# Beginning the second pair's value loads three places sooner in a macaron block with local attention

## The chip, the cores and the metric

The kernel runs on one core of a Trainium2 chip. The metric is the device time of one execution in microseconds (us), lower is better. A measured time is the median of several executions; beside it stands one execution that the hardware profiler recorded, from which every duration below comes.

A core has five engines with a queue of instructions each: PE (TensorE, matrix products; its weight loads are listed as PEld), DVE (VectorE), ACT (ScalarE), POOL (GpSimd) and SP (SyncE, which in this kernel only issues DMA transfers). Each works through its own queue in order, and waits where an instruction needs what another has not finished. Sixteen DMA engines carry out the transfers.

## The reference

The input is four sequences of 4096 rows of 512 numbers in float32. Each goes through three residual stages, with a layer norm ahead of each:

```python
x = x + 0.5 * ffn(layernorm(x))          # rows and weights rounded to a 6-bit grid per 32 numbers
x = x + attention(layernorm(x))
x = x + 0.5 * ffn(layernorm(x))
```

The attention has 16 heads of 32 numbers. Each row attends to the 13 rows around it only (at the ends of a sequence, to the 13 nearest the end), with a bias that depends on the relative position:

```python
attn = einsum('bhld,bhlkd->bhlk', q, k[nbr]) + rpb[:, bidx]
out = einsum('bhlk,bhlkd->bhld', softmax(attn), v[nbr])   # then out @ proj_w.T + proj_b
```

## The kernel before

**Tiles, groups, steps.** The rows are 128 tiles of 128. Four tiles make a group, so there are 32 groups, eight to a sequence. A float32 factor of a product is kept as two float16 parts, high and low, and a product is three sweeps of four matmuls of 128x512 (`product`, line 151): 12 matmuls. One step of the steady part does one tile of each stage, for different tiles: the first half-step `ffn` and the second (PSUM tiles `pmf`), the values (`pmv`), a quarter of a group's queries and keys (`pmqk`, two products), the scores (`ps`, line 433), the weighted sums (`pv`, line 503) and the output projection (`pmo`).

**Slots.** The order of the work is written out by hand. `begin(slot, stage, rank)` puts a stage in a slot; `run_slot` runs the stages of a slot by rank and moves each to its next slot, as its `yield slots, rank` says. A step is `STEP = 7` slots. What a stage emits in a slot goes to the end of the engines' queues, so slots and ranks alone set the order in every queue, SP's included.

**Scores and values.** The queries of a group are cut in blocks of 30; a block sees 42 keys. A block's probabilities, with high and low parts side by side, are transposed by a DMA (`pT<-p`, line 485) and multiplied with stacked values: 42 rows of v high, again v high, and v low, one over the other, for each block. [...] v goes through DRAM: `values` (line 299) computes a tile of v, ACT and DVE split it into `vt` (lines 310 and 311), and SP writes it out (`vd<-vt`, line 312). Once a group's rows are in DRAM, `load_stack` (line 394) reads them back, block by block (`vs<-vd`, line 409). It is called twice for a group: a pair is the 256 columns of eight heads, so pair 0 and pair 1 together are a group's 512 columns. A call issues three DMAs (high, high, low), or six in the first and last group of a sequence, where a block at the end breaks the even spacing. The pool `vsp` has two buffers; pair 1 of a group takes the one of pair 1 of the group before, so its loads wait until PE has read that.

**What else SP issues in a step.** Three transposes, one after another: `pT<-p`, `xT<-hlq` (line 205; the quantised rows for an `ffn` product, both halves together) and `x<-hln` (line 205; the normed rows for queries, keys and values). Then the write of v, the output of a finished tile (`out_dram<-x`, line 555) and the load of a new input tile (line 176). Each DMA of SP counts on one of eight semaphores in turn, so it also waits for the DMA eight places ahead of it to have landed.

**Where the two calls of `load_stack` stand.** Pair 0 is begun in slot 6*7+4 after the group's start, rank 9: behind the transposes of that step. Pair 1 is begun in slot 8*7, rank 9: the slot in which the next step's `values` stage issues its write of v, with rank 7.

Below, a group's four steps are counted from the first score matmul of each: pair 0's loads are issued near the end of the first step, pair 1's at the change from the second step to the third.

Of the kernel before, what the change touches and what calls it, by code (L numbers as in the profile page):

```python
# [64 lines left out]
def macaron_kernel(  # L65
# [96 lines left out]
    def begin(slot, stage, rank=5):  # L162
        slots.setdefault(slot, []).append((rank, stage))
# [395 lines left out]
    STEP = 7  # L559
# [6 lines left out]
    def one(f, *args):  # L566
        f(*args)
        return
        yield
# [22 lines left out]
    for t in range(NT):  # L592
        k = t * STEP
# [16 lines left out]
    for m in range(n_items):  # L610
        k = m * STEP
# [3 lines left out]
    for n in range(n_batch * NG):  # L615
        k = n * GROUP * STEP
        b, g = divmod(n, NG)
        begin(k + 6 * STEP + 4, one(load_stack, b, g, 0), 9)
        begin(k + 8 * STEP, one(load_stack, b, g, 1), 9)


    with tc.tile_pool(name="setup", bufs=1) as sp, tc.tile_pool(name="scratch", bufs=2) as scr:
# [289 lines left out]
```

## Time and profile before

| | |
|---|---|
| time before, median of 3 runs | 2408.76 us (2407.12 to 2414.85) |
| the profiled execution's own time | 2401.24 us |
| its span in the profile | 2399.4 us |
| granted TensorE clock, mean | 0.993 |
| busy: PE, DVE, POOL, ACT | 95%, 84%, 83%, 55% |
| DMA traffic | 360.58 MB, 150 GB/s in the mean |
| loads of stacked values (`vs<-vd`) | 144 of 357.0 KB, 24 of 378.0 KB, 24 of 315.0 KB, 48 of 21.0 KB |

The span is the profiler's stretch from the first to the last instruction. An entry such as "pmf<-wt,xT" names the tile written and those read. A wait is put down to what ended it; "issue" means that the profile shows nothing that the engine waited for. The chain of waits follows the work that ended last back to its beginning. In a timeline of SP, the length is the time that SP took to issue the DMA, not the transfer. The trace also holds each DMA packet and each increment of a DMA's semaphore, from which a landing time is read.

### The profile page before, as it was taken

The page shows a single profiled execution, that of the slowest core. Times are in us where ns is not written, and L with a number is a line of the kernel's source. Part 1 is how long each engine was busy: PE and PEld are TensorE (multiplying, and loading weights), DVE is VectorE, ACT ScalarE, POOL GpSimd, SP SyncE. Part 2 cuts the span into 40 slices and gives each one's busy share as a digit, 9 for nine tenths or more (in the row PEclk, how much of TensorE's full clock was granted, in tenths as well). Part 3 has the DMA queues.
Part 4 walks back from the last instruction along what each step waited for, and adds up shares of the span by engine and source line. Part 5 has one row for each costly group of instructions (what it writes and reads, how often), then busy time and mean ns, then how long its engine had stood idle before and what let it go on. Part 6 is the DMA issues. An engine that isn't in the chain of part 4 may idle for free.

```text
span 2399.4 us, 82333 instructions
## 1 busy us (share of the span) xinstructions
PE 2278.8 (95%) x35539; PEld 1114.0 (46%) x35539; DVE 2015.3 (84%) x3588; ACT 1327.1 (55%) x2080; POOL 1989.0 (83%) x2012
## 2 busy tenths in 40 slices
PE   0799999999999999999999999999999999999987
PEld 0244444444444444444444444444444444444442
DVE  8789888888888888888888888888888888888775
ACT  4455555555555556555555555555555555555442
POOL 5578888888888888888888888888888888888677
PEclk9899999999999999999999999999999999999998
DMA  5788888787787877778867778777778887777753
GB/s 153 145 150 153 158 164 158 148 157 151 145 161 156 152 150 159 146 153 162 161 145 156 150 146 167 153 154 147 159 139 156 158 158 146 162 148 143 137 115 90
DMA packets 925700, 360.58 MB, mean 150 GB/s; under 512 B 718876, under 2 KB 889752, under 8 KB 925336
## 3 DMA queue, kind: packets, MB, share of 16 engines
q1 hardware_dynamic: 924992, 354.79, 75.6%
q8 instruction: 278, 4.55, 0.8%
q10 hardware_dynamic: 344, 0.53, 0.1%
q14 instruction: 86, 0.70, 0.1%
HBM read 110.15 MB, written 67.29 MB: 74 GB/s over the span
## 4 chain that ended last, share of the span: by engine, by line
PE 89%; DVE 4%; DMA 3%; issue 1%; POOL 1%; ACT 1%; SPq 0%; DVEq 0%; ACTq 0%; POOLq 0%
PE pmqk L151 27%; PE pmf L151 26%; PE pmo L151 14%; PE pmv L151 13%; PE ps L433 6%; PE pv L503 3%; DMA xT<-hlq 2%; DVE hlq L204 0%; DVE fw L749 0%; DMA x<-hln 0%; DVE qk L373 0%; DVE stn L180 0%; POOL x L564 0%; ACT ring L530 0%; DVE whl L779 0%
## 5 line engine op out<-in xcount | busy, mean ns | idle before, releaser
L151 PE MATMUL pmf<-wt,xT 128*128 128x512 f16 x3048 | 703.1, 381 | 17.8 <-DMA xT<-hlq 17.7
L151 PE MATMUL pmqk<-x,wt 128*128 128x512 f16 x3072 | 707.7, 380 | 6.2 <-DMA x<-hln 5.4
L151 PEld LDWEIGHTS <-xT 128*128 128x128 f16 x3048 | 297.0, 98 | 386.1 <-DMA xT<-hlq 29.3
L151 PEld LDWEIGHTS <-wt 128*128 128x128 f16 x3072 | 290.0, 98 | 343.1 <-issue 9.7
L151 PE MATMUL pmv<-wt,x 128*128 128x512 f16 x1536 | 353.8, 380 | 5.1 <-DMA x<-hln 5.1
L151 PE MATMUL pmo<-wt,ring 128*128 128x512 f16 x1536 | 355.3, 381 | 2.6 <-issue 2.6
L246 POOL TENSOR_TENSOR yq<-yq,r 128x1024 f32<-128x1024 f32 (+1 forms) x141 | 246.2, 1746 | 130.8 <-DVE r L244 130.8
L564 POOL TENSOR_TENSOR x<-x,half_ffn_b 128x512 f32<-128x512 f32 x256 | 327.4, 1279 | 0.1
L275 DVE SCALAR_TENSOR_TENSOR x<-pmf,coef,x 128x512 f32<-128x512 f32 x256 | 179.5, 701 | 165.2 <-PE pmf L151 164.7
L530 ACT ACTIVATE ring<-pv 128x510 f16<-128x510 f32 (+8 forms) x224 | 82.3, 414 | 400.5 <-PE pv L503 400.5
L310 ACT CAST vt<-pmv 128x512 f16<-128x512 f32 x128 | 74.9, 585 | 389.3 <-PE pmv L151 389.3
L180 DVE BATCH_NORM_STATS2 stn<-x 128x6 f32<-128x512 f32 x384 | 265.3, 691 | 8.9 <-DMA x<-in_L_attn_x_dram 0.2
L251 POOL TENSOR_TENSOR yq<-q,sc 128x1024 f32<-128x1024 fp8e4 (+1 forms) x141 | 246.7, 1749 | 0.4 <-ACT q L249 0.4
L151 PEld LDWEIGHTS <-x 128*128 128x128 f16 x1536 | 150.5, 98 | 187.6 <-DMA x<-hln 5.6
L373 DVE SCALAR_TENSOR_TENSOR qk<-pmqk,qk_b,qk 128x512 f16<-128x512 f32 x256 | 190.6, 744 | 53.8 <-ACT qk L369 53.0
L476 POOL TENSOR_TENSOR sf<-sf,total 128x714 f32<-128x714 f32 (+2 forms) x128 | 178.6, 1395 | 44.2 <-DVE total L474 25.0
L151 PEld LDWEIGHTS <-ring 128*128 128x128 f16 x1536 | 140.2, 98 | 161.5 <-issue 4.2
L186 POOL TENSOR_SCALAR rsq<-mv 128x2 f32<-128x2 f32 (+1 forms) x141 | 131.3, 931 | 96.0 <-DVE mv L181 93.8
L249 ACT ACTIVATE q<-yq,nudge 128x1024 fp8e4<-128x1024 f32 (+1 forms) x141 | 149.9, 1063 | 108.0 <-POOL yq L246 99.8
L369 ACT ACTIVATE qk<-pmqk,qk_b 128x512 f16<-128x512 f32 x256 | 176.1, 688 | 53.2 <-PE pmqk L151 52.1
L233 ACT ACTIVATE yq<-x,nbq,rsq 128x512 f32<-128x512 f32 x254 | 193.0, 804 | 20.8 <-POOL nbq L192 20.2
L467 POOL TENSOR_TENSOR sf<-sf,top 128x714 f32<-128x714 f32 (+2 forms) x128 | 180.4, 1409 | 20.0 <-DVE top L465 19.8
(145 smaller groups left out, 3466.9 us busy)
## 6 DMA issues: line engine op xcount, KB each, us to landing
vs<-vd SPq DMA_DIRECT2D x144, 357.0 KB
x<-in_L_attn_x_dram SPq DMA_DIRECT2D x128, 256.0 KB
vd<-vt SPq DMA_DIRECT2D x128, 256.0 KB
out_dram<-x SPq DMA_DIRECT2D x128, 256.0 KB
vs<-vd SPq DMA_DIRECT2D x24, 378.0 KB
vs<-vd SPq DMA_DIRECT2D x24, 315.0 KB
rows<-in_L_attn_qkv_w_dram SPq DMA_DIRECT2D x12, 256.0 KB
xT<-hlq SPq DMA_TRANSPOSE x141
```

The source lines that it names most:

```text
L151: nc.tensor.matmul(pm, lhs(a, c), rhs(b, c), start=(n == 0), stop=(n == 3 * KC - 1))
L180: nc.vector.bn_stats(st, xs[t])
L233: nc.scalar.activation(y[:, u], xs[t], AF.Identity, bias=nb[:, u : u + 1], scale=rs[:, u : u + 1])
L246: nc.gpsimd.tensor_tensor(yb, yb, bc(r, QB), ALU.mult)
L249: nc.scalar.activation(q8, y, AF.Identity, bias=nudge, saturate=False)
L251: nc.gpsimd.tensor_tensor(yb, q8.rearrange("p u (n q) -> p (u n) q", q=QB), bc(sc, QB), ALU.mult)
L275: nc.vector.scalar_tensor_tensor(xs[t], pm, cf, xs[t], ALU.mult, ALU.add)
L369: nc.scalar.activation(t[:, s, 0, KN:], pms[s], AF.Identity, bias=bias)
L373: nc.vector.scalar_tensor_tensor(t[:, s, 1, KN:], pms[s], bias, t[:, s, 0, KN:], ALU.add, ALU.subtract)
L467: nc.gpsimd.tensor_tensor(s, s, bc(top[:, :n], KN), ALU.subtract)
L476: nc.gpsimd.tensor_tensor(s, s, bc(total[:, :n], KN), ALU.mult)
L564: nc.gpsimd.tensor_tensor(xs[t], xs[t], b, ALU.add)
```

## The change

The call of `load_stack` for pair 1 is begun in slot 7*7+4 after the group's start instead of slot 8*7. Rank, loads, buffers and all other stages are as they were.

```diff
         k = n * GROUP * STEP
         b, g = divmod(n, NG)
         begin(k + 6 * STEP + 4, one(load_stack, b, g, 0), 9)
-        begin(k + 8 * STEP, one(load_stack, b, g, 1), 9)
+        begin(k + 7 * STEP + 4, one(load_stack, b, g, 1), 9)
```

In SP's queue the order of a group's third step's beginning changes from `pT, xT, hln, vd, vs vs vs, out, x` to `pT, xT, hln, vs vs vs, vd, out, x`, with these names for the transposes of probabilities, quantised rows and normed rows, the write of v, the three loads, the output and the input load.

## The prediction

> **What bounds the kernel now.** The page first: its span, TensorE's (PE's) busy line, and the queue that brings instructions.
>
> ```profile
> span 2399.4 us, 82333 instructions
> PE 2278.8 (95%) x35539; PEld 1114.0 (46%) x35539; DVE 2015.3 (84%) x3588; ACT 1327.1 (55%) x2080; POOL 1989.0 (83%) x2012
> q8 instruction: 278, 4.55, 0.8%
> ```
>
> PE sets the end, and away from the two ends of the run it hardly ever stops. So a moved load can only give back what PE still waits, and take what it newly waits. Next, then, the waits of PE alone between 200 and 2270 us, where the steps are all alike (columns: us in total, times, longest):
>
> ```profile
> PE pmf L151 <- DMA xT<-hlq: 7.1, 9, 1.6
> PE ps L433 <- issue: 3.3, 3, 1.8
> PE pv L503 <- issue: 3.1, 5, 1.2
> PE pmo L151 <- issue: 2.6, 2, 2.1
> PE pmqk L151 <- issue: 0.8, 2, 0.5
> ```
>
> That is 16.9 us in all: 7.1 us for the transposed quantised rows xT, and 9.8 us of "issue", for which the profile names no releaser. To place them, I take one group's four steps as windows (columns: stretch, its length, PE, PEld, DVE, ACT and POOL busy, clock, DMA share, GB/s):
>
> ```profile
> 1008.20:1025.80 17.60, 17.60 (x283) 8.67 (x286) 15.17 (x27) 10.17 (x17) 15.23 (x17) 1.00 0.80 174
> 1025.80:1043.80 18.00, 17.80 (x285) 8.76 (x288) 15.16 (x27) 10.22 (x18) 15.30 (x17) 1.00 0.71 133
> 1043.80:1061.40 17.60, 17.60 (x288) 8.67 (x291) 15.23 (x26) 10.04 (x16) 15.18 (x16) 1.00 1.00 186
> 1061.40:1079.00 17.60, 17.60 (x288) 8.66 (x291) 15.09 (x26) 10.12 (x17) 15.26 (x17) 1.00 0.59 123
> ```
>
> A step, counted from its first score matmul, is 17.60 us of PE work; DVE and POOL have 2.4 us to spare in it. The third step is the one with full DMA engines (1.00), the fourth the emptiest. The SP queue in order of time says why (start, length of the issue):
>
> ```profile
> 1017.87 1.74 SPq L205 DMA_TRANSPOSE x<-hln  x1
> 1019.71 1.64 SPq L409 DMA_DIRECT2D vs<-vd  x3
> ...
> 1035.53 1.70 SPq L205 DMA_TRANSPOSE x<-hln  x1
> 1042.58 0.38 SPq L312 DMA_DIRECT2D vd<-vt  x1
> 1043.05 1.57 SPq L409 DMA_DIRECT2D vs<-vd  x3
> 1044.73 1.99 SPq L555 DMA_DIRECT2D out_dram<-x  x1
> ...
> 1048.34 4.85 SPq L485 DMA_TRANSPOSE pT<-p  x1
> 1053.29 2.96 SPq L205 DMA_TRANSPOSE xT<-hlq  x1
> ```
>
> The first pair's loads (1019.71) come right behind the last transpose of the first step. The second pair's (1043.05) come behind the write of v, which waits for DVE until 1042.58, so they stand just ahead of the third step's transposes: there pT takes 4.85 us to issue. Over steps 8 to 115 of the trace the issue of pT averages 5.21 us in third steps and 2.54 to 2.57 us in the others; xT is issued 9.99 us into the step instead of 7.75 to 7.90, and lands at 15.05 instead of 12.51 to 12.86. The pmf product that reads it wants to start at 14.93 to 15.05. That is the wait for xT, and every one of them in the steady part is in a third step.
>
> **The change part by part.** Nothing is computed differently and PE's order is unchanged; on SP 114 loads in 31 groups (three a group, six at the ends of a sequence) move past one instruction, the write of v. The last group has no such write, and keeps its order.
>
> *a. The third step's transposes.* The loads are begun behind x<-hln, at about 1037.3 (1035.53 + 1.70) instead of 1043.05: 5.7 us sooner. The second step's end is then what the first step's end is now, where loads follow the transposes directly; the step after those has its xT at 12.69, 2.3 us ahead of need. So the wait should go. Its size: 7.1 us by the matmuls' row above; counted from start to start of the matmuls against 0.22 us each, 9.0 us, since part of it shows on the weight loads. I take 9.0 (bounds 7.1 and 11).
>
> *b. The "issue" waits.* Every one of them in the window ends 2.3 to 2.9 us after a q8 packet starts, so I read them as PE waiting for code. q8 brought 278 packets of 16,384 bytes; PE's 71,078 instructions divided by 278 are 256 each. They fall in second and third steps only, that is, after loads. The third step's six are in pv, 2.9 us in all counted from start to start, at 6.9 to 7.5 us into the step, behind a packet that started only at 4.0 to 4.7; in second steps, where the loads are older, packets start at 2 to 3.6. With the change the third step is like the second, so these go: -2.9 us (bounds 0 and 2.9).
>
> *c. What comes instead.* Second steps have their own code waits. Numbering PE's instructions in blocks of 256, they occur when the step's first score matmul stands 124 to 184 into its block: eight second steps in the window, with 0.43, 0.67, 0.58, 2.29, 0, 0, 0.35 and 1.51 us, in sum 5.8, mean 0.73. Third steps stand in that band eight times too (131, 132, and twice each at 140, 152, 180). Now they lose nothing there to code but wait for xT; changed, they should pay 8 x 0.73 = 5.8 us. [...] The row has 9.8 us of exposed waits that end with a packet, so I take 5.8 and keep zero as the lower end. The upper end is the last group, whose two pairs already follow transposes directly, in two steps on end; from the chain of waits:
>
> ```profile
> 2296.49 1.50 issue
> ...
> 2310.74 2.42 issue
> ```
>
> The longer one in each of 10 third steps (the band with its two neighbours at 188) is 24 us.
>
> *d. Start-up.* In the first group, the second pair's six loads are issued from 142.26, pT blocks behind them, x<-hln is issued at 153.83, and the chain of waits holds PE until it lands:
>
> ```profile
> 153.83 4.27 DMA x<-hln
> ```
>
> PE stands from 152.8 to 158.1. The transpose before the loads ends at 140.14, so they start 2.1 us sooner, and pT, xT and x<-hln with them: -2.0 us (bounds 0 and -4, as the third group's end of start-up, a 1.79 us "issue" at 209.75, may shrink as well).
>
> *e. At no cost.* The loads also wait for PE to have read the old values in their buffer: that pv ends at 1033.3, four us before 1037.3. Were that cover gone, SP would stand, and the v write, output, input load and next pT behind it. The v write now issues after three loads (1.6 us), but waits for DVE until 1042.58 anyway, by when they are out; on the engines it lands behind them, as in the first step, at 21.1 instead of 19.1 us from the second step's start. Who reads it is the next group's load, over two steps on, and its buffer is written again two steps on. The output and the input load come free of the loads: the latter lands at about 6.0 instead of 9.96 in the third step. DVE, ACT and POOL get nothing new. The loaded values are first read three steps later.
>
> Sum: -9.0 - 2.9 + 5.8 - 2.0 = -8.1 us, against the profiled execution's own 2401.24 us (span 2399.4): 2393.1. The runs shown have a median of 2408.76, 7.5 us above the profiled one; I put the same difference on it: 2400.7.
>
> **The rivals.** *The gain without the price (2394.9):* code comes in time because the loads are out when the next step's scores are reached. For it: packets of first and fourth steps, which have no loads before them, cost nothing. Against it: second steps. *Nothing moves (2408):* the DMA work is the same, and with less than 17 us of waits the runs' own spread (2407.12 to 2414.85) is nearly as large; it would be so if xT is late for another reason. Against it: xT is late by 2.2 us only in third steps, exactly where pT's issue is 2.7 us longer. *Slower:* two sets of loads now end two steps in succession, and the third step's score matmuls (128 with as many weight loads, a whole block of code in 1.2 us) meet the loads' tail. The place is ps in the third step, the price up to 2.42 us each. Ten are 24.2 us, less 13.9 of gains: +10.3, 2419. It decides from 13.9 us of new "issue" in third steps, 1.4 us in each of the ten; for it speaks the last group, against it the mean of 0.73 in second steps.
>
> **How the numbers follow.** The forecast has 0.50 (2396 to 2405: c between 1.5 and 10 us), the gain without price 0.12, nothing 0.18, slower 0.20. About 0.3%, 7.2 us, is what a measurement of this kernel can tell from no change; the forecast's own spread lies across that line, 0.32 beyond it and 0.18 within. Faster: 0.32 + 0.12 + 0.02 = 0.46. Same: 0.18 + 0.14 + 0.02 = 0.34. Slower: 0.18 + 0.02 = 0.20. The range goes from the gain without price and a larger d (2391) to half-way into the slower case (2415).
>
> **What would show it.** a: no pmf wait for xT in third steps, pT's issue there near 2.6 us, xT landing near 12.7. b: no pv "issue". c: "issue" in ps, pmo or pmqk of third steps, about 6 us. d: the chain's x<-hln near 154 is 2 us shorter. DMA share of the third step falls from 1.00 towards 0.75 and the second's rises. The prediction is wrong if "issue" grows by more than the xT wait shrinks, or if xT is still late.

## The result, and the profile after

The changed kernel takes 2403.31 us (median of 22 runs, 2392.93 to 2418.35) against 2412.06 us before, measured beside it (22 runs, 2407.12 to 2418.33). The ratio is 0.9964, 95% interval 0.9952 to 0.9977: faster by 8.7 us. The forecast was 8.1 us.

The recorded execution of the changed kernel is its slowest: 2418.35 us, span 2416.6. That is 15 us above its median, so its sum can't be set against the one before. Its parts can, with care; a second profile, nearer to the median, follows below. First, PE's waits between 200 and 2270 us (in total, times, longest):

```profile
PE pmo L151 <- issue: 12.5, 5, 3.6
PE ps L433 <- issue: 10.7, 6, 4.5
PE pmqk L151 <- issue: 1.1, 2, 0.8
PE pv L503 <- issue: 1.0, 1, 1.0
```

The wait for xT (7.1 us before) is gone. The waits with no releaser have grown from 9.8 to 25.3 us, and they are longer: 4.5 us against 2.1. The SP queue at the change from a second to a third step (start, length of the issue):

```profile
1038.27 1.67 SPq L205 DMA_TRANSPOSE x<-hln  x1
1040.05 1.88 SPq L409 DMA_DIRECT2D vs<-vd  x3
1046.11 0.39 SPq L312 DMA_DIRECT2D vd<-vt  x1
1048.14 0.36 SPq L555 DMA_DIRECT2D out_dram<-x  x1
1048.55 0.47 SPq L176 DMA_DIRECT2D x<-in_L_attn_x_dram  x1
1051.48 2.25 SPq L485 DMA_TRANSPOSE pT<-p  x1
1054.94 2.91 SPq L205 DMA_TRANSPOSE xT<-hlq  x1
```

The loads now follow x<-hln, and pT is issued in 2.25 us where it took 4.85. Over steps 8 to 115, pT's issue in third steps takes 2.52 us in the mean where it took 5.21, and xT lands 13.2 us into the step; it was 15.05.

One of the long waits, from the chain of waits of the same profile:

```profile
824.01 1.25 PE ps L433 x131
825.26 4.55 issue
829.81 0.28 PE ps L433 x4
830.09 5.07 PE pmo L151 x12
```

Twelve pmo matmuls take 5.07 us behind that wait; in the undisturbed steps of the profile before they take 2.70. The granted clock is the reason: the trace shows it at 0.5 for 6.8 us from 828 us on. In the whole steady part this profile has five such stretches, of 3.4 or 6.8 us, each behind a wait for no named releaser; the profile of before has none there.

Last the start-up, by the chain of waits and by PE's own wait between 116 and 225 us; first as before, then changed (the landing of the first group's x<-hln, and the product behind it):

```profile
153.83 4.27 DMA x<-hln
...
158.15 4.44 PE pmqk L151 x12
PE pmqk L151 <- DMA x<-hln: 4.1, 1, 4.1
```

```profile
152.21 3.78 DMA x<-hln
155.99 0.04 issue
156.03 2.75 PE pmqk L151 x12
PE pmqk L151 <- DMA x<-hln: 1.2, 1, 1.2
```

The product starts 2.1 us sooner, and takes 1.7 us less. Before, the granted clock is 0.5 for 3.4 us from 158.4 us on, behind the wait of 4.1 us; changed, behind a wait of 1.2 us, it stays at 1.

### The profile page after: what moved, and what is told of

Its sections match the earlier page's. It is cut to its first block, busy times and chain, and to the rows that moved or that the text cites. A ratio compares the mean times of both kernels' runs of the same rounds, so it can differ in the third digit from the quotient of the medians.

```text
span 2416.6 us, 82362 instructions
## 1 busy us (share of the span) xinstructions
PE 2288.2 (95%) x35539; PEld 1117.5 (46%) x35539; DVE 2016.4 (83%) x3588; ACT 1327.0 (55%) x2080; POOL 1987.7 (82%) x2012
## 3 DMA queue, kind: packets, MB, share of 16 engines
q8 instruction: 278, 4.55, 0.8%
## 4 chain that ended last, share of the span: by engine, by line
PE 91%; DVE 4%; issue 2%; DMA 1%; POOL 1%; ACT 0%; SPq 0%; DVEq 0%; POOLq 0%; ACTq 0%
PE pmqk L151 28%; PE pmf L151 26%; PE pmo L151 14%; PE pmv L151 13%; PE ps L433 6%; PE pv L503 3%; DVE hlq L204 0%; DVE fw L749 0%; DMA x<-hln 0%; DVE stn L180 0%; DMA x<-in_L_attn_x_dram 0%; DVE whl L779 0%; POOL x L564 0%; DMA xT<-hlq 0%; DVE sc L239 0%
## 5 line engine op out<-in xcount | busy, mean ns | idle before, releaser
L151 PE MATMUL pmo<-wt,ring 128*128 128x512 f16 x1536 | 367.9, 390 | 19.0 <-issue 18.9
L249 ACT ACTIVATE q<-yq,nudge 128x1024 fp8e4<-128x1024 f32 (+1 forms) x141 | 149.9, 1063 | 109.0 <-POOL yq L246 100.8
```

The lines of the kernel that those rows point to most:

```text
L151: nc.tensor.matmul(pm, lhs(a, c), rhs(b, c), start=(n == 0), stop=(n == 3 * KC - 1))
L249: nc.scalar.activation(q8, y, AF.Identity, bias=nudge, saturate=False)
```

## The experiments

The changed kernel is the base; a short diff stands for each edit. For each profile the table gives what PE lost in steps 8 to 123, 29 of each kind, counted from start to start of its matmuls: waits for xT, waits with no releaser ("code", see the second experiment), and the excess of matmuls at half clock. First steps are left out: they lose 0.6 us to code with the second pair alone, 0.2 us with all six loads spread, and nothing elsewhere. "First eight" is the time from the first score matmul to that of the ninth step. A row is one execution. All in us.

| kernel | time of the profiled execution | first eight | second steps: xT / code / half clock | third steps: xT / code / half clock | fourth steps: code / half clock |
|---|---|---|---|---|---|
| before | 2401.2 | 108.3 | 0 / 7.2 / 0 | 9.0 / 2.9 / 0 | 0 / 0 |
| before, again | 2411.2 | 109.9 | 0 / 7.7 / 1.6 | 9.2 / 4.3 / 0 | 0 / 0 |
| changed | 2418.4 | 103.7 | 0 / 13.2 / 3.0 | 0 / 12.8 / 6.1 | 0 / 0 |
| changed, again | 2400.5 | 102.7 | 0 / 6.3 / 1.6 | 0 / 10.4 / 3.8 | 0 / 0 |
| start-up alone moved | 2407.0 | 106.1 | 0 / 8.1 / 0 | 9.3 / 5.4 / 0 | 0.2 / 0 |
| all but the start-up moved | 2411.8 | 109.0 | 0 / 7.4 / 0 | 0 / 13.1 / 4.4 | 0 / 0 |
| second pair one step later | 2389.3 | 100.2 | 0 / 6.0 / 1.9 | 0 / 0 / 0 | 6.3 / 1.6 |
| both pairs behind v's write | 2428.1 | 114.3 | 10.7 / 9.3 / 3.1 | 6.3 / 10.3 / 1.6 | 0 / 0 |
| no loads | 2375.4 | 104.9 | 0 / 0 / 0 | 0 / 0.3 / 0 | 0.6 / 0 |
| second pair alone loaded | 2386.3 | 106.9 | 0 / 0 / 0 | 0 / 8.7 / 0 | 0 / 0 |
| second pair's loads singly | 2382.0 | 100.2 | 0 / 6.8 / 0 | 0 / 0 / 0 | 0 / 0 |
| all six loads spread | 2372.1 | 100.2 | 0 / 1.5 / 0 | 0 / 0.9 / 0 | 0.8 / 0 |

**The changed kernel, and the one before, once more.** No edit; a second profile of each.

> The changed kernel once more, timed beside the one before, for a second profile of it. Theory (third step's transposes freed, code waits in second and third steps): 0.996 of before again; no wait for xT in third steps; code waits about 6 us each in second and third steps in a usual execution, and more, with a halved clock behind the long ones, in an execution as slow as the first profile (2418 us). Rival (the gain is in the start-up alone): the first eight steps about 4 us shorter, and the 116 steps behind them no shorter than before in an execution near the median.

> The kernel before once more, for a second profile: the first one was 2401 us where the median is 2408. Expected: the same waits for xT in third steps, 7 to 10 us; more code waits than the 10 us of the first profile if the execution is a longer one, most of them in second steps.

The changed kernel: 0.9975 of before (0.9966 to 0.9984), 2402.86 us in the median, its profile close to that. PE's waits in it, same view and window as above:

```profile
PE pmo L151 <- issue: 8.1, 4, 3.5
PE ps L433 <- issue: 5.4, 6, 3.7
PE pv L503 <- issue: 1.2, 2, 0.9
```

The kernel before: profiled at 2411.18 us, with the wait for xT as expected. The table's first four rows then say what the slowest execution couldn't: the change takes 9.0 to 9.2 us of waits for xT out of third steps, and puts code waits of 10.4 to 12.8 us with 3.8 to 6.1 us of half clock in the place of 2.9 to 4.3. Third steps so pay more for code than the 6 us expected. The third step as a whole is no shorter. What is shorter in both profiles of the changed kernel is the first eight steps: 102.7 and 103.7 us against 108.3 and 109.9. The 116 steps behind them take 2059.7 and 2072.7 us changed, and 2057.1 and 2061.2 before: no shorter, as the rival had it. In the slowest execution second steps, too, lose more, 16.2 us against 7.9 in the other one; why was not found.

**The loads left out.** What do the loads cost, and do the waits without a releaser come from them?

```diff
         st = vsp.tile([P, MAXB, 2 * P], F16, tag="vs", name=f"vs{b}_{g}_{pair}")
-        stacks[b, g, pair] = st
+        stacks[pair] = st
+        nc.gpsimd.memset(st, 0.0)
+        return
...
+        if n:
+            continue
         begin(k + 6 * STEP + 4, one(load_stack, b, g, 0), 9)
```

> Leaves out the loads of stacked values altogether: the two stacks are zeroed once and read throughout, so the attention's output is wrong and its time is that of a kernel without these loads. Theory (code waits and xT's wait both come from the loads): code waits in the steady steps fall to nearly nothing, no wait for xT, no halved clock, a step of 17.60 us throughout: 20 to 30 us less than before, 0.988 to 0.992. Rival (code waits come from PE's own pace through its code, the loads do not matter): code waits stay near 10 us, 0.994 to 0.996.

0.9866 (0.9848 to 0.9884), a little more gain than expected. Its waits of PE, same view and window:

```profile
PE pmo L151 <- issue: 2.3, 3, 1.6
PE pmf L151 <- DMA xT<-hlq: 0.8, 1, 0.8
```

In the steady steps 0.9 us of these waits is left, so the loads are the cause of nearly all of them. That PE waits for code is read from the traces in two ways. With PE's instructions in the trace numbered in order of their start, the twelve profiles of this document hold 127 "issue" waits of PE between 200 and 2270 us, and every one ends at an instruction whose number is 193 or 194 past a multiple of 256. And in the eleven profiles with loads, 123 of 124 end 2.3 to 3.2 us after a 16 KiB packet of the instruction queue had started, one 3.9 us after. The packets themselves are late behind the loads: counted from number 150 past the multiple of 256, about where the earliest ones start, the mean delay to the packet's start is 1.5 us without the loads (at most 3.9) and 2.4 us in the profile before (at most 10.0). What in the DMA engines holds them up is not shown. In steps 8 to 123 PE lost 0.9 us to code without the loads, 10.1 and 12.0 in the two profiles before, and 26.0 and 16.7 in the two of the changed kernel.

**Start-up and steady part apart.**

```diff
-        begin(k + 7 * STEP + 4, one(load_stack, b, g, 1), 9)
+        begin(k + (7 * STEP + 4 if n < 2 else 8 * STEP), one(load_stack, b, g, 1), 9)
```

```diff
-        begin(k + 7 * STEP + 4, one(load_stack, b, g, 1), 9)
+        begin(k + (8 * STEP if n < 2 else 7 * STEP + 4), one(load_stack, b, g, 1), 9)
```

> Only the first two groups' second pairs are moved, the other 30 stay as before: the start-up part of the change alone. Theory: the start-up is 4 to 6 us shorter (both profiles of the changed kernel show it), all else as before: 0.9975 to 0.9985 of before. Rival (the start-up is the whole gain): the same ratio as the changed kernel. If the gain lies in the steady steps, as the prediction had it (2 of 8 us in the start-up): 0.999.

> The complement: the first two groups stay as before, the others are moved. By the prediction's sum 6 of its 8 us: 0.9975. Rival (the start-up is the whole gain, what xT's wait gives back in the steady steps is eaten by code waits): 1.000.

The first two groups alone give 0.9974 (0.9959 to 0.9989), 6.3 us of 2412.63; the other groups alone 0.9990 (0.9977 to 1.0004), 2.4 us with an interval from 5.5 us faster to 1 us slower. So most of the gain is in the start-up. Whether the steady part gives anything is not settled: the interval holds both, and the third step's sum in the table (17.5 us, against 11.9 and 13.5 before) speaks against. Nor does the profile with the start-up alone moved show the gain where the changed kernel has it:

```profile
152.03 4.75 DMA x<-hln
156.79 0.04 issue
156.83 4.38 PE pmqk L151 x12
```

Its six loads took 5.05 us to issue, where they took 2.92 in the changed kernel. PE still waits 3.9 us for x<-hln, and the product still runs at half clock. The first eight steps are 2.2 and 3.8 us shorter than in the two profiles before, most of it in the eighth step; the changed kernel's are 4.6 to 7.2 us shorter. So the size of the gain in the start-up differs from execution to execution.

PE's waits with all but the start-up moved:

```profile
PE pmo L151 <- issue: 9.7, 4, 4.4
PE ps L433 <- issue: 7.9, 6, 4.0
PE pmqk L151 <- issue: 1.3, 3, 0.6
PE pv L503 <- issue: 1.2, 1, 1.2
```

They are those of the changed kernel: no xT, long code waits.

**The suspected cost, doubled.** Both pairs behind a write of v.

```diff
-        begin(k + 6 * STEP + 4, one(load_stack, b, g, 0), 9)
-        begin(k + 7 * STEP + 4, one(load_stack, b, g, 1), 9)
+        begin(k + 7 * STEP, one(load_stack, b, g, 0), 9)
+        begin(k + 8 * STEP, one(load_stack, b, g, 1), 9)
```

> Both pairs behind a write of v: the first pair's loads put where the second pair's stood before, one step ahead, and the second pair's left where they stood. The suspected cost, doubled. Theory: pT and xT of the second step are late by 2 us as well, 9 us of waits for xT in second steps added, against the code waits of second steps that turn milder (7 to 3 us): 1.001 to 1.004 of before. Rival (the place in the step does not matter): 1.000.

1.0095 (1.0074 to 1.0115), slower by far more than expected. PE's waits for xT, same view and window:

```profile
PE pmf L151 <- DMA xT<-hlq: 10.8, 11, 2.1
```

By the table's count, which takes in what of a wait shows on the weight loads, the second step now pays 10.7 us for xT, as the theory said: its pT takes 5.2 us to issue and xT lands at 15.4. But its code waits grew to 9.3, where I had expected 3, those of the third step grew to 10.3, and the start-up is 4 to 6 us longer. Loads ahead of the transposes do delay them; they don't make code waits mild.

**One step later.** The second pair behind the third step's transposes.

```diff
-        begin(k + 7 * STEP + 4, one(load_stack, b, g, 1), 9)
+        begin(k + 8 * STEP + 4, one(load_stack, b, g, 1), 9)
```

> The second pair's loads one step later still, behind the third step's transposes: as free of the transposes as in the changed kernel, and not in the step right after the first pair's. Theory: xT's wait stays away, as in the changed kernel; code waits move from third to fourth steps at about the same size: 0.995 to 0.998 of before. Rival (two sets of loads in steps on end make the long code waits): fewer code waits than in the changed kernel, 0.992 to 0.995. If only the distance to the third step's transposes counted and nothing of the place: equal to the changed kernel.

0.9917 (0.9898 to 0.9935): better than the changed kernel, and just under the rival's range. The fourth step's code waits and half clock are 6.3 and 1.6 us, where the third step of the changed kernel paid 10.4 and 3.8 or more. The first eight steps are shorter again (100.2).

**The second pair alone.** The first pair's stack is zeroed once and never loaded, so half of the attention's output is left out.

```diff
+        if pair == 0 and (0, 0, 0) in stacks:
+            stacks[b, g, 0] = stacks[0, 0, 0]
+            return
-        st = vsp.tile([P, MAXB, 2 * P], F16, tag="vs", name=f"vs{b}_{g}_{pair}")
+        st = vsp.tile([P, MAXB, 2 * P], F16, tag=f"vs{pair}", bufs=1, name=f"vs{b}_{g}_{pair}")
         stacks[b, g, pair] = st
+        if pair == 0:
+            nc.gpsimd.memset(st, 0.0)
+            return
```

> The changed kernel with the first pair's loads left out (its stack is zeroed once and read throughout, so half of the attention's output is wrong); the second pair's loads stand where the change puts them. It asks why the third step pays more for code (14 to 19 us with the halved clock) than the second (8). Theory (two sets of loads in steps on end): alone, the third step pays 8 us or less. Rival (the place in the code, as long waits are hit where a block of code ends within the scores): the third step still pays 14 to 19 us. In both cases the second step pays nearly nothing; 0.988 to 0.992 of before if 8, 0.992 to 0.996 if 14 to 19.

0.9894 (0.9865 to 0.9923). PE's waits, same view and window:

```profile
PE pmo L151 <- issue: 6.1, 4, 2.5
PE ps L439 <- issue: 2.2, 3, 1.0
PE pmqk L151 <- issue: 0.6, 1, 0.6
```

The third step pays 8.7 us for code, a little more than the theory's 8, and nothing for the clock; the longest wait is 2.5 us. The loads stand in the same place and PE's code is the same; without the first pair's loads one step ahead, the longer waits are gone. With the run one step later (a step between the two sets, 7.9 us behind each) this says that the third step's price in the changed kernel comes from two sets of loads in steps on end. It rests on one profile of each, and does not explain the second steps of the slowest execution, which lost 16.2 us behind one set. How the first set reaches into the step after next (the second step being late, or what it leaves in the queues) was not told apart.

**The second pair one load at a time.**

```diff
-        begin(k + 7 * STEP + 4, one(load_stack, b, g, 1), 9)
+        begin(k + 7 * STEP + 4, one(load_stack, b, g, 1, (0,)), 9)
+        begin(k + 8 * STEP + 4, one(load_stack, b, g, 1, (1,)), 9)
+        begin(k + 9 * STEP + 4, one(load_stack, b, g, 1, (2,)), 9)
```

(`load_stack` gets the parts as an argument, and takes a new tile with part 0.)

> The first pair's three loads in one go in the first step, as before; the second pair's one at a time, behind the transposes of the second, third and fourth step. Theory (the length of the queue of loads makes the code wait): second steps still pay about 8 us for code, third and fourth steps less than 2 us each: 0.987 to 0.990 of before. Rival (any load ahead of the scores costs a wait): third and fourth steps pay 5 us or more each, 0.993 to 0.998.

0.9884 (0.9857 to 0.9912). Second steps, behind the first pair's three loads, pay 6.8 us; third and fourth steps, behind one load each, pay nothing. The second pair's loads move the same bytes as before, so it is the number of loads in one go that makes code late.

**All six spread.**

```diff
-        begin(k + 6 * STEP + 4, one(load_stack, b, g, 0), 9)
-        begin(k + 7 * STEP + 4, one(load_stack, b, g, 1), 9)
+        begin(k + 6 * STEP + 4, one(load_stack, b, g, 0, (0, 1)), 9)
+        begin(k + 7 * STEP + 4, one(load_stack, b, g, 0, (2,)), 9)
+        begin(k + 8 * STEP + 4, one(load_stack, b, g, 1, (0, 1)), 9)
+        begin(k + 9 * STEP + 4, one(load_stack, b, g, 1, (2,)), 9)
```

> The six loads of a group are spread over its four steps, always behind the transposes: two of the first pair in the first step and one in the second, two of the second pair in the third and one in the fourth. Theory (a code wait is the longer, the more loads are queued in one go): bursts of two and one instead of three leave shorter code waits; less than 10 us in all and hardly a halved clock: 0.985 to 0.990 of before, faster than with the second pair as one burst in the third step (0.992). Rival (any loads before the scores cost a code wait): waits in all four steps, 0.992 to 0.998.

0.9848 (0.9830 to 0.9867), 2372.65 us in the median, in a range of 2.4 us: faster than both kernels, with all the work done, and no slower than the kernel without loads (2375.42 us, in another series). Its waits of PE, same view and window:

```profile
PE ps L435 <- issue: 1.3, 2, 0.7
PE pmo L151 <- issue: 1.2, 2, 0.7
```

No xT, 2.5 us of code waits where the changed kernel's two profiles had 25.3 and 14.7, no half clock in the steady part.

## Why the prediction was right or wrong

The total was right, 8.1 us against 8.7 in one series and 6.0 in another (0.9975 of 2408.39), but in good part by luck. Two of its terms were not right, and their errors offset each other: 6.1 us were to come from the steady steps and 2.0 from the start-up, and the two parts, moved singly, gave 2.4 (between 5.5 faster and 1 slower) and 6.3 (2.7 to 9.9).

*a, the third step's transposes: right.* 9.0 us foreseen, 9.0 and 9.2 measured in the two profiles before, all of it gone in every profile in which these loads do not stand ahead of the transposes. The DMA share of the third step fell from 1.00 to 0.78 in the group around 1050 us and that of the second rose from 0.71 to 0.84, as foreseen.

*b, pv's code waits: right.* 2.9 us foreseen; 2.9 and 4.3 us of third-step code waits in the two profiles before, and in the changed kernel's third steps of the steady part none is in pv but one of 0.45 us.

*c, the new code waits: right in kind, size wrong.* 5.8 us foreseen, by carrying the second step's mean of 0.73 us over to the third. Measured with the halved clock: 14.2, 17.5 and 18.9 us in three profiles. Two things were left out. A third step follows two sets of loads and not one; alone it pays 8.7 us. And a long wait can be paid twice, as the clock can fall behind it (3.8, 4.4 and 6.1 us of the three sums are half clock); the profile before, from which the mean was taken, had no half clock in the steady part, though in the other profile before one second step's wait of 2.2 us had it. The rival "slower" had the mechanism, two sets of loads in succession, and put it at 24 us; the measured price lies between the two. By the prediction's own sign it was wrong in the first profile, where "issue" grew by 15.5 us and the wait for xT shrank by 7.1; in the second "issue" grew by 4.9 us only, to 14.7. No profile with these loads moved shows the zero that the prediction kept as the lower end, and on which its rival's 2394.9 rests: the least of the three is 14.2 us.

*d, the start-up: size wrong.* 2.0 us foreseen, 6.3 measured (2.7 to 9.9). In the changed kernel x<-hln came 2.1 us sooner, as worked out. PE did not stand from 152.8 to 158.1, though: the scores run from 152.7 to 154.0, and the wait is the 4.1 us of the row above. Left out was that the product behind that wait ran at half clock: 1.7 us more, in plain sight in the chain's 4.44 us for twelve matmuls. The fourth step of the start-up fell from 18.28 to 14.23 and 14.38 us in the two profiles. The rest is in the eighth step, where a code wait shrank (17.2 and 18.8 us before, 16.7 and 15.5 changed); it stood among the bounds as possible. With the start-up alone moved it was the other way round: the fourth step stayed at 18.1 us and the eighth fell to 15.3. So which of the two gives the gain isn't fixed.

*e, at no cost: held.* The loads issue right behind x<-hln, with no wait for PE before them, and the v write waits for DVE as before.

*The rivals.* "The gain without the price" did not come with this change; it is what spreading the loads gives. "Nothing moves" is nearly the truth for the steady steps, but not for its reason: xT was late because of the loads; another wait took the place.

## What to carry to other kernels

In this long unrolled program a burst of DMA loads held up the transposes behind it, at 9.0 to 9.2 us of waits for xT before, and also the code: PE lost 26.0 and 16.7 us in the changed kernel's two profiles to waits for which the profile names no releaser, against 0.9 without the loads. Look for "issue" waits that end with a packet of the instruction queue, and spread the burst over the steps before choosing its place (here that left 3.2 us of such waits in the same steps). And where PE waits for some microseconds, look at the matmuls behind the wait too: if they take twice their usual time (5.07 us against 2.70 behind the wait of 4.55), the wait's price is larger than its length.

## What the runs showed of the hardware

The instruction queue q8 brought 278 packets of 16 KiB in the profile before, for 71,078 instructions of PE, so I count 256 to a packet; in 123 of the 124 "issue" waits of the profiles with loads PE went on 2.3 to 3.2 us after such a packet had started, and so I call them waits for code. With three loads of 357 KB queued in one go, the steps behind lost 6 to 9 us per 29 steps to code, 13.2 in the slowest execution, and 2.9 to 5.4 in the third steps of the kernel before and of the one with the start-up alone moved; with two 0.8 to 1.5, with one 0 to 0.9, with none 0 to 0.6; with two sets in steps on end 10 to 13.

The granted clock changes between 1 and 0.5 only, and in each of the twelve profiles all its changes stand whole multiples of 3.41 us apart, to 0.005 us. With the time between 200 and 2270 us cut at these places, 14 pieces at full clock have PE idle for 2.08 us or more, and after each the clock is 0.5; after none with 1.60 us or less it is, and of 16 between these it is after five. So a wait of a given length can halve the clock or not, as it falls: with the second pair alone waits of 2.49 and 2.45 us left it at 1, as at most 2.00 and 1.90 us of them lie in one piece.

The changed kernel's first 22 runs cover 25 us, those with spread loads 2.4 (five runs) and those without loads 1.7 (four). The spread went down with the code waits, as far as so few runs can say.
